# A two-layer graph network on one core: the table of k laid out by type, and key codes loaded for two blocks at once

## The chip, the cores and the metric

The kernel runs on one core of a Trainium2 chip. The core has five engines with an instruction queue each: TensorE (PE, matrix products, with its weight loads shown as PEld), VectorE (DVE), ScalarE (ACT), GpSimd (POOL) and SyncE (SP), which here only issues transfers. Sixteen DMA engines carry all transfers. A transfer is issued from the queue of SP or ACT (in the profile the hardware queues q1 and q10) or, where the addresses come from a list of row numbers, by POOL (an indirect transfer, queue q0). The metric is the time of one execution on the device in microseconds, lower is better.

## The reference

There are N = 30,000 nodes with 128 numbers each, and E = 960,000 edges (src, dst) sorted by destination. Layer 0 is a pair of relational convolutions, layer 1 a gated convolution with four edge types:

```python
# layer 0: 32 edge types, weights combined from 8 bases
W   = einsum('rb,bdf->rdf', coeff, basis)
msg = einsum('nd,rdf->nrf', h, W)[src, etype] * norm
agg = segment_sum(msg, dst)            # twice, relu between; x = x + result
# layer 1: T = 4 edge types
for t in range(T):
    k, q, v = x @ Wk[t] + bk[t], x @ Wq[t] + bq[t], x @ Wv[t] + bv[t]
    msg = sigmoid(k[dst] + q[src]) * v[src]
    msg = where(edge_type == t, msg, 0)
    outs.append(segment_sum(msg, dst) + x @ Ws[t] + b[t])
return x_in + mean(outs)               # x here is relu(layernorm(x_in))
```

## The kernel before

The kernel checks first that the destinations are sorted closely enough; then `sorted_path` runs (the other branch, `any_path`, is in the program but is not executed with these inputs). It passes over all edges three times: c1 and c2 for the two convolutions of layer 0, g for the gate of layer 1. A pass works on groups of 384 edges (three tiles of 128), 2500 of them. Five groups are a block (S = 5), five blocks a stage, twenty stages an iteration of 500 groups, and a hardware loop does five iterations. Because edges are sorted, the destinations of one group lie in a window of W = 32 consecutive nodes; `first` holds where each window starts. The sums stand in SBUF as `agg`, feature by node.

Between c2 and g the kernel does not stop: while c2 goes on, `after_second` takes finished nodes, 120 at a time, and writes for each node the four types' k (with the biases of k and q added) into the DRAM table `ktab`, and q and v into `qvtab` (stores at L817 from ACT, 480 rows of 512 bytes and 480 rows of 1024 bytes). In `ktab` the row of node n and type t is n * 4 + t, so a window of 32 nodes is 128 consecutive rows. During c1, `codes` writes two lists for the gate: `qidx` (src * 4 + type, the rows to gather from `qvtab`) and `kcode` (node within the window * 4 + type, bfloat16, one per edge; L890).

The gate pass (`gate_body`) does this for each group n:

- three indirect gathers by POOL, of 128 rows of 1 KB each, fetch q and v of the edges' sources into `qv` (L119, ten groups' buffers). A gather is issued when the buffer of ten groups before has been read;
- SP loads the window of k, 64 KB, into `kw` (L651, ten buffers), five groups ahead of the group that POOL is at; its start comes from a register that SP read from `first`;
- three products by PE of a one-hot matrix `oh` with `kw` give each edge its k, `pk` (`keys`, L668); they are issued one group ahead;
- DVE adds q (L709), ACT takes the sigmoid in place (L710), DVE multiplies by v two groups later into `msg` (L677), and three products by PE with the selection matrix `sel` sum the messages by window (L679);
- once per block, DVE makes the next block's `oh` (L655, 128 x 1920, from the key codes `kb`, comparing them with the partition's number) and `sel` (L661), and adds the last block's windows into `agg` (L470).

`kb` holds the key codes of one block, broadcast to all 128 partitions by a load of 480 KB (L644, 128 rows of 3840 bytes, two buffers). It is issued at the first group of block s for block s + 1 and takes the place of block s - 1's codes, last read by the `oh` that DVE makes at group 1 of block s - 2. At the first group of a stage, SP also loads `qi` (row numbers for POOL), `relc` and `firsts` for the next stage. Every ten groups a node step copies finished sums out (`after_third`: L846 on ACT, L850 on PE, L853 on ACT, store L856).

The order on each queue is written out by hand (`manual_schedule`); waits between engines are semaphores that the framework derives. The gathers use five semaphores in turn, and a gather waits for the one five before it. Within SP's queue, kw loads, kb loads and stage loads stand in program order, and SP runs ahead of the other engines as far as the buffers allow.

The first pass has a load of a similar shape: `er`, the types of a block's edges, is read with an outer dimension of four, a broadcast over 32 and 2 KB rows (L512, 256 KB).

Of the kernel before, what the change touches and what calls it, by code (L numbers as in the profile page):

```python
# [9 lines left out]
F32 = mybir.dt.float32  # L10
# [9 lines left out]
P = 128  # L20
# [53 lines left out]
def kernel(  # L74
# [33 lines left out]
    h1 = nc.dram_tensor("h1", (NX, D), F32, kind="Internal").ap()  # L108
    agg1 = nc.dram_tensor("agg1", (NA, D), F32, kind="Internal").ap()
    agg2 = nc.dram_tensor("agg2", (NA, D), F32, kind="Internal").ap()  # L110
    ktab = nc.dram_tensor("ktab", (NX * T, D), F32, kind="Internal").ap()
    qvtab = nc.dram_tensor("qvtab", (NX * T, 2 * D), F32, kind="Internal").ap()
    reld = nc.dram_tensor("reld", (TP, NT), F32, kind="Internal").ap()
    kcode = nc.dram_tensor("kcode", (E,), BF16, kind="Internal").ap()
# [205 lines left out]
    def node_tables(pool, ps, wall, ball, hn, krows, qvrows):  # L320

        pt = ps.tile([P, P], F32, name="pt")
        nc.tensor.transpose(pt, hn, ident)
        hT = pool.tile([P, P], F32, name="hT")
        nc.scalar.activation(hT, pt, AF.Relu)
        kt = pool.tile([P, T, D], F32, name="kt")
        qvt = pool.tile([P, T, 2, D], F32, name="qvt")
        to = (kt, qvt[:, :, 0, :], qvt[:, :, 1, :])
        for a in range(3):
            pw = ps.tile([P, T, D], F32, name="pw", bufs=4)  # L330
            nc.tensor.matmul(pw.rearrange("p t f -> p (t f)"), lhsT=hT,
                             rhs=wall[:, a].rearrange("p t f -> p (t f)"), start=True, stop=True)
# [4 lines left out]
        nc.scalar.dma_start(krows, kt.rearrange("p t f -> p (t f)"))  # L337
        nc.sync.dma_start(qvrows, qvt.rearrange("p t a f -> p (t a f)"))
        return hT

    knode = ktab.rearrange("(n t) f -> n (t f)", t=T)
    qvnode = qvtab.rearrange("(n t) f -> n (t f)", t=T)


    def sorted_path():
# [7 lines left out]
        with ExitStack() as all_:  # L353
# [105 lines left out]
                    min_val=0, max_val=N - 1, skip_runtime_bounds_check_because=IN_RANGE)  # L459
                return vals  # L460

            def edge_row(row, i, s, n):

                return bass.AP(tensor=row.tensor, offset=(i * NG + s * S) * GE,
                               ap=[[0, n], [GE, S], [1, GE]])

            def add_windows(po, base, s, at=0):
                for g in range(S):
# [164 lines left out]
            def gate_body(i, io, pool, ps, cp, iw, ic, beside):  # L633
                stage = {}
                kb, oh, kw, sel, pk, qv, po, base, kbase = {}, {}, {}, {}, {}, {}, {}, {}, {}

                def loads(k):
                    got = [stage_tile(io, "qi", qidx, I32, i, k), firsts(io, i, k),
                           stage_tile(io, "relc", reld, F32, i, k)]
                    stage[k] = [got[1], got[0], got[2]]  # L640

                def types(s):
                    kb[s] = pool.tile([P, S, GE], BF16, name="kb")
                    nc.sync.dma_start(kb[s], edge_row(kcode, i, s, P))  # L644

                def window(n):
                    k = n // NGS
                    if n % NGS == 0:
                        kbase[k] = bases(stage[k][0], SP)
                    kw[n] = pool.tile([P, D], F32, name="kw", bufs=10)  # L650
                    nc.sync.dma_start(kw[n], ktab[ds(kbase[k][n % NGS] * T, P), :])  # L651

                def onehot(s):
                    oh[s] = pool.tile([P, S, GE], F32, name="oh")
                    nc.vector.tensor_tensor(oh[s], kb[s],  # L655
                                            ic.unsqueeze(2).to_broadcast([P, S, GE]),
                                            ALU.is_equal)
                    sel[s] = pool.tile([TP, S * G, W], F32, name="sel", bufs=3)
                    t0 = s % SB * S * G
                    relc = stage[s // SB][2][:, t0:t0 + S * G]  # L660
                    nc.vector.tensor_tensor(  # L661
                        sel[s], iw[:TP].unsqueeze(1).to_broadcast([TP, S * G, W]),
                        relc.unsqueeze(2).to_broadcast([TP, S * G, W]), ALU.is_equal)

                def keys(n):
                    pk[n] = ps.tile([TP, G, D], F32, name="pk", bufs=4)
                    for j in range(G):
                        nc.tensor.matmul(pk[n][:, j, :],  # L668
                                         lhsT=oh[n // S][:, n % S, j * TP:(j + 1) * TP],
                                         rhs=kw[n], start=True, stop=True)  # L670

                def sums(n):
                    s, g = n // S, n % S
                    if g == 0:
                        po[s] = ps.tile([P, S, W], F32, name="po")
                    msg = pool.tile([TP, G, D], F32, name="msg", bufs=3)
                    nc.vector.tensor_mul(msg, pk[n], qv[n][:, :, 1, :])  # L677
                    for j in range(G):
                        nc.tensor.matmul(po[s][:, g, :], lhsT=msg[:, j, :],  # L679
                                         rhs=sel[s][:, g * G + j, :],  # L680
                                         start=(j == 0), stop=(j == G - 1))

                loads(0)
                types(0)
                for n in range(S):
                    window(n)
                onehot(0)
                keys(0)
                for n in range(NG):
                    s, g, k = n // S, n % S, n // NGS  # L690
                    if n % NGS == 0:
                        if k in BEGINS:
                            tc.stage_boundary()
# [13 lines left out]
                    if n + 1 < NG:  # L707
                        keys(n + 1)
                    nc.vector.tensor_add(pk[n], pk[n], qv[n][:, :, 0, :])  # L709
# [12 lines left out]
                add_windows(po[NS - 1], base[NQ - 1], NS - 1)  # L722
# [36 lines left out]
            def after_second(weights):  # L759

                def steps(at, pool, ps, deep):
# [63 lines left out]
                    def own():  # L825
# [6 lines left out]
                            (7, biased(1, qvt[:, :, :D])), (7, weight(2)), (7, part),  # L832
                            (8, biased(2, qvt[:, :, D:])), (8, own),
                            (9, store(nc.sync if isinstance(at, int) else nc.scalar,
                                      qvnode, qvt)))
                return steps

            def after_third(weights):
# [22 lines left out]
            def codes(i, pool):  # L861
# [8 lines left out]
                def part(h):  # L870
# [38 lines left out]
    def any_path():  # L909
        with ExitStack() as all_:  # L910
# [112 lines left out]
            with tc.tile_pool(name="snodew", bufs=1) as nodew, \  # L1023
# [8 lines left out]
                with tc.For_i(0, NB, 1) as i:  # L1032
                    xt = node.tile([P, 1, D], F32, name="xt")
                    nc.sync.dma_start(xt[:, 0, :], agg2[ds(i * P, P), :])
                    hn = normalised(node, xt, 1, "snode")
                    hT = node_tables(node, nps, wall, ball, hn[:, 0, :], knode[ds(i * P, P), :],
                                     qvnode[ds(i * P, P), :])
                    po = nps.tile([P, D], F32, name="po")
                    nc.tensor.matmul(po, lhsT=hT, rhs=wsm, start=True, stop=True)
# [5 lines left out]
            with tc.tile_pool(name="gslow", bufs=2) as pool, \  # L1045
# [7 lines left out]
                nc.vector.scalar_tensor_tensor(ki, di, float(T), e4, op0=ALU.mult, op1=ALU.add)  # L1053
                k = pool.tile([TP, G, D], F32, name="k")
                qv = pool.tile([TP, G, 2 * D], F32, name="qv")
                for j in range(G):
                    gather(qv[:, j, :], qvtab[:NP * T, :], qi[:, j:j + 1])
                    gather(k[:, j, :], ktab[:NP * T, :], ki[:, j:j + 1])
# [80 lines left out]
```

## Time and profile before

Ten runs: median 33253.57 us (33241.48 to 33262.07). The profiled execution took 33250.78 us.

| What | us |
|---|---|
| profiled execution, its own time | 33250.78 |
| its span, first to last instruction | 33248.9 |
| first pass, first to last gather | 159 to 11029 |
| second pass | 11055 to 21847 |
| gate pass | 21886 to 33225 |
| POOL busy, whole span | 21332.0 (64%) |
| PE busy | 19752.3 (59%) |
| PE weight loads | 16299.6 (49%) |
| DVE busy | 11504.8 (35%) |
| ACT busy | 3590.1 (11%) |

In the profile's lines, `out<-in` names the tiles of the program, `x` a number of instructions, and after `<-` stands what ended an engine's wait. "issue" means that the profile shows nothing that was waited for, "remote" that the release came from a semaphore event with no instruction's end near it. SPq and ACTq are the queues that issue transfers. The times of PE's matmuls are modelled, so PE's real completions are read from what waits for them.

### The profile page before, as it was taken

The page shows a single profiled execution, that of the slowest core. Times are in us where ns is not written, and L with a number is a line of the kernel's source. Part 1 is how long each engine was busy: PE and PEld are TensorE (multiplying, and loading weights), DVE is VectorE, ACT ScalarE, POOL GpSimd, SP SyncE. Part 2 cuts the span into 40 slices and gives each one's busy share as a digit, 9 for nine tenths or more (in the row PEclk, how much of TensorE's full clock was granted, in tenths as well). Part 3 has the DMA queues.
Part 4 walks back from the last instruction along what each step waited for, and adds up shares of the span by engine and source line. Part 5 has one row for each costly group of instructions (what it writes and reads, how often), then busy time and mean ns, then how long its engine had stood idle before and what let it go on. Part 6 is the DMA issues. An engine that isn't in the chain of part 4 may idle for free. (4 is left out here: it accounts for less than half of the span.)

```text
span 33248.9 us, 278474 instructions
## 1 busy us (share of the span) xinstructions
PE 19752.3 (59%) x79371; PEld 16299.6 (49%) x79371; DVE 11504.8 (35%) x23672; ACT 3590.1 (11%) x9806; POOL 21332.0 (64%) x22514
## 2 busy tenths in 40 slices
PE   4555555555555566666666666655555555555565
PEld 3444444444444444444444444445555555555555
DVE  4333333333333333333333333333333333333333
ACT  2000000000000111111111111111111111111111
POOL 5666666666666666666666666666666666666666
PEclk8777777777777787887888888865555555555555
DMA  3222222222222222222222222234444444444444
GB/s 110 65 65 71 65 70 66 65 72 65 68 68 65 64 67 66 67 68 66 66 67 67 67 66 67 67 107 126 125 125 126 125 126 126 124 126 126 125 126 121
DMA packets 1982877, 2920.57 MB, mean 88 GB/s; under 512 B 680564, under 2 KB 1364077, under 8 KB 1981277
## 3 DMA queue, kind: packets, MB, share of 16 engines
q0 software_dynamic: 840000, 1967.52, 22.0%
q1 hardware_dynamic: 740695, 661.98, 6.8%
q10 hardware_dynamic: 400582, 272.46, 2.8%
q8 instruction: 672, 11.01, 0.1%
q14 instruction: 928, 7.60, 0.1%
HBM read 2626.82 MB, written 273.30 MB: 87 GB/s over the span
## 5 line engine op out<-in xcount | busy, mean ns | idle before, releaser
L119 POOL DMA_INDIRECT hg<-h,idx x15000 | 14194.7, 946 | 7624.1 <-issue 4203.4
L605 PE MATMUL pa<-sb,hg 128*128 128x256 f32 x30000 | 9110.0, 460 | 6472.0 <-issue 5223.7
L605 PEld LDWEIGHTS pa<-sb,hg 128*128 128x128 f32 x30000 | 6737.2, 234 | 8568.0 <-issue 5906.3
L119 POOL DMA_INDIRECT qv<-qvtab,qi x7500 | 7110.1, 948 | 4268.0 <-issue 2054.9
L679 PE MATMUL po<-sel,msg 128*128 128x32 f32 x15000 | 3455.8, 386 | 4568.6 <-DVE msg L677 4174.0
L679 PEld LDWEIGHTS po<-sel,msg 128*128 128x128 f32 x15000 | 3429.1, 328 | 4854.3 <-DVE msg L677 4330.8
L668 PE MATMUL pk<-kw,oh 128*128 128x128 f32 x15000 | 3998.4, 439 | 57.1 <-DVE oh L655 46.8
L609 ACT COPY ab<-pa 128x256 f32<-128x256 f32 x5000 | 1802.2, 373 | 19528.6 <-remote 9954.2
L709 DVE TENSOR_TENSOR pk<-pk,qv 128x384 f32<-128x384 f32 x2500 | 1406.5, 563 | 7026.4 <-remote 4728.8
L668 PEld LDWEIGHTS pk<-kw,oh 128*128 128x128 f32 x15000 | 3478.8, 331 | 57.7 <-issue 57.7
L470 DVE TENSOR_TENSOR agg<-agg,pb 128x32 f32 x5000 | 937.8, 188 | 6491.9 <-remote 5369.3
L555 PE MATMUL pb<-ab,bas 128*128 128x160 f32 (+1 forms) x12080 | 2571.9, 369 | 554.9 <-ACT ab L609 358.6
L555 PEld LDWEIGHTS pb<-ab,bas 128*128 128x128 f32 x12080 | 2071.3, 205 | 1046.6 <-issue 406.1
L601 DVE TENSOR_TENSOR sb<-cp,ce 128x768 f32<-128x768 f32 x2500 | 2320.8, 949 | 693.8 <-remote 496.5
L601 DVE TENSOR_TENSOR sb<-hits,ce 128x768 f32<-128x768 f32 x2500 | 2294.9, 951 | 255.0 <-issue 164.9
L710 ACT ACTIVATE pk<-pk 128x384 f32<-128x384 f32 x2500 | 1187.3, 475 | 7700.6 <-DVE pk L709 4720.2
L801 PE MATMUL bank<-wall,hT 128*120 128x512 f32 x1518 | 975.5, 762 | 893.9 <-ACT hT L797 376.7
L677 DVE TENSOR_TENSOR msg<-pk,qv 128x384 f32<-128x384 f32 x2500 | 1369.7, 548 | 11.7 <-remote 10.2
L784 DVE BATCH_NORM_STATS2 st<-bank 120x6 f32<-120x128 f32 x253 | 75.6, 299 | 3321.6 <-remote 1489.1
L655 DVE TENSOR_TENSOR oh<-kb,cp 128x1920 f32<-128x1920 bf16 x500 | 1072.5, 2145 | 21.8 <-DMA kb<-kcode 15.8
L801 PEld LDWEIGHTS bank<-wall,hT 128*120 128x120 f32 x1518 | 324.9, 227 | 1190.9 <-issue 502.1
L812 DVE TENSOR_TENSOR kt<-bank,ball 120x512 f32<-120x512 f32 x253 | 175.0, 692 | 1775.1 <-PE bank L801 776.6
(83 smaller groups left out, 5486.2 us busy)
## 6 DMA issues: line engine op xcount, KB each, us to landing
hg<-h,idx POOLq DMA_INDIRECT x15000
kb<-kcode SPq DMA_DIRECT2D x500, 480.0 KB
kw<-ktab SPq DMA_DIRECT2D x2500, 64.0 KB
er<-in_et_row SPq DMA_DIRECT2D x500, 256.0 KB
qvtab<-qvt ACTq DMA_DIRECT2D x250, 480.0 KB
qv<-qvtab,qi POOLq DMA_INDIRECT x7500
ktab<-kt ACTq DMA_DIRECT2D x253, 240.0 KB
ce<-ce ACTq DMA_DIRECT2D x500, 60.0 KB
```

The costliest lines, as they stand in the source:

```text
L119: nc.gpsimd.indirect_dma_start(out=to, out_offset=None, in_=table, in_offset=bass.IndirectOffsetOnAxis(ap=idx, axis=0))
L555: nc.tensor.matmul(po[z][:, of].rearrange("p s w -> p (s w)"), lhsT=bas[:, b, :], rhs=ab[z][:, b, of].rearrange("p s w -> p (s w)"), start ...
L601: nc.vector.tensor_mul(sb, hits[:, of, :].unsqueeze(2).to_broadcast([TP, G, B, W]), ce[s][:, of, :].unsqueeze(3).to_broadcast([TP, G, B, W]))
L605: nc.tensor.matmul(pa.rearrange("p b w -> p (b w)"), lhsT=hg[:, j, :], rhs=sb[:, j].rearrange("p b w -> p (b w)"), start=(j == 0), stop=(j ...
L609: nc.scalar.copy(ab[z][:, :, s % A * S + g, :], pa)
L655: nc.vector.tensor_tensor(oh[s], kb[s], ic.unsqueeze(2).to_broadcast([P, S, GE]), ALU.is_equal)
L668: nc.tensor.matmul(pk[n][:, j, :], lhsT=oh[n // S][:, n % S, j * TP:(j + 1) * TP], rhs=kw[n], start=True, stop=True)
L677: nc.vector.tensor_mul(msg, pk[n], qv[n][:, :, 1, :])
L679: nc.tensor.matmul(po[s][:, g, :], lhsT=msg[:, j, :], rhs=sel[s][:, g * G + j, :], start=(j == 0), stop=(j == G - 1))
L709: nc.vector.tensor_add(pk[n], pk[n], qv[n][:, :, 0, :])
L710: nc.scalar.activation(pk[n], pk[n], AF.Sigmoid)
L801: nc.tensor.matmul(bank(a, VB, T * D), lhsT=hT, rhs=wall[:, a].rearrange("p t f -> p (t f)"), start=True, stop=True)
```

## The change

Two things change in the gate pass, and the tables it reads change with them.

- `ktab` becomes a table of four planes, type then node: (T, NX, D) instead of (NX * T, D). A window load reads, for each of the four types, 32 consecutive nodes, so the source of `kw` has three dimensions, 4 x 32 x 128, and partition t * 32 + w of `kw` holds type t of window node w. The store of k writes each node's four rows into four planes. The key code becomes type * 32 + node within the window, which is made by the same DVE operation with its two operands exchanged.
- `kb` holds the codes of two blocks. It is loaded at the first group of every even block, for the pair of blocks after, as 128 rows of 7680 bytes (960 KB), and each block's one-hot reads its half.

```diff
-    ktab = nc.dram_tensor("ktab", (NX * T, D), F32, kind="Internal").ap()
+    ktab = nc.dram_tensor("ktab", (T, NX, D), F32, kind="Internal").ap()
...
-    knode = ktab.rearrange("(n t) f -> n (t f)", t=T)
+    knode = ktab.rearrange("t n f -> n t f")
...
-            def edge_row(row, i, s, n):
+            def edge_row(row, i, s, n, groups):
                 return bass.AP(tensor=row.tensor, offset=(i * NG + s * S) * GE,
-                               ap=[[0, n], [GE, S], [1, GE]])
+                               ap=[[0, n], [GE, groups], [1, GE]])
...
-                def types(s):
-                    kb[s] = pool.tile([P, S, GE], BF16, name="kb")
-                    nc.sync.dma_start(kb[s], edge_row(kcode, i, s, P))
+                def types(z):
+                    kb[z] = pool.tile([P, 2 * S, GE], BF16, name="kb")
+                    nc.sync.dma_start(kb[z], edge_row(kcode, i, 2 * z, P, 2 * S))
...
-                    nc.sync.dma_start(kw[n], ktab[ds(kbase[k][n % NGS] * T, P), :])
+                    nc.sync.dma_start(kw[n], ktab[:, ds(kbase[k][n % NGS], W), :])
...
-                    nc.vector.tensor_tensor(oh[s], kb[s],
+                    nc.vector.tensor_tensor(oh[s], kb[s // 2][:, s % 2 * S:s % 2 * S + S],
                                             ic.unsqueeze(2).to_broadcast([P, S, GE]),
                                             ALU.is_equal)
...
-                    if g == 0 and s + 1 < NS:
-                        types(s + 1)
+                    if g == 0 and s % 2 == 0 and s + 2 < NS:
+                        types(s // 2 + 1)
...
-                            queue.dma_start(
-                                table[rows, :].rearrange("p (t f) -> p t f", t=T), t)
+                            queue.dma_start(table[rows], t)
...
-                        nc.vector.scalar_tensor_tensor(kc, kr, float(T), er, op0=ALU.mult,
+                        nc.vector.scalar_tensor_tensor(kc, er, float(W), kr, op0=ALU.mult,
                                                        op1=ALU.add)
```

The rest of the diff is the same layout in `any_path`, which is not executed.

More of the change, by code (lines that the diff above doesn't have):

```diff
@@ L336, in node_tables @@
                 nc.vector.tensor_add(to[a], pw, ball[:, a])
-        nc.scalar.dma_start(krows, kt.rearrange("p t f -> p (t f)"))
+        nc.scalar.dma_start(krows, kt)
         nc.sync.dma_start(qvrows, qvt.rearrange("p t a f -> p (t a f)"))
         return hT
-    knode = ktab.rearrange("(n t) f -> n (t f)", t=T)
+    knode = ktab.rearrange("t n f -> n t f")
     qvnode = qvtab.rearrange("(n t) f -> n (t f)", t=T)
@@ L834, in steps @@
                             (9, store(nc.sync if isinstance(at, int) else nc.scalar,
-                                      qvnode, qvt)))
+                                      qvnode.rearrange("n (t f) -> n t f", t=T), qvt)))
                 return steps
@@ L1035, in any_path @@
                     hn = normalised(node, xt, 1, "snode")
-                    hT = node_tables(node, nps, wall, ball, hn[:, 0, :], knode[ds(i * P, P), :],
+                    hT = node_tables(node, nps, wall, ball, hn[:, 0, :], knode[ds(i * P, P)],
                                      qvnode[ds(i * P, P), :])
@@ L1052, in any_path @@
                 ki = pool.tile([TP, G], I32, name="ki")
-                nc.vector.scalar_tensor_tensor(ki, di, float(T), e4, op0=ALU.mult, op1=ALU.add)
+                nc.vector.scalar_tensor_tensor(ki, e4, float(NX), di, op0=ALU.mult, op1=ALU.add)
                 k = pool.tile([TP, G, D], F32, name="k")
@@ L1057, in any_path @@
                     gather(qv[:, j, :], qvtab[:NP * T, :], qi[:, j:j + 1])
-                    gather(k[:, j, :], ktab[:NP * T, :], ki[:, j:j + 1])
+                    gather(k[:, j, :], ktab.rearrange("t n f -> (t n) f"), ki[:, j:j + 1])
                 s = pool.tile([TP, G, D], F32, name="s")
```

## The prediction

> **What bounds the kernel now.** I read the page first, then the three passes over the edges as three stretches, then the gate pass alone: the order of its instructions around one block, and what the queue of SP waits for.
>
> The costliest groups of the page; after the bar come busy time, mean of one, and the idle time ahead of it:
>
> ```profile
> L119 POOL DMA_INDIRECT hg<-h,idx x15000 | 14194.7, 946 | 7624.1 <-issue 4203.4
> L119 POOL DMA_INDIRECT qv<-qvtab,qi x7500 | 7110.1, 948 | 4268.0 <-issue 2054.9
> ```
>
> The three passes (stretch, its length, then busy time of PE, weight load, DVE, ACT, POOL; granted clock; DMA share; GB/s):
>
> ```profile
> 159.00:11029.00 10870.00, 6193.28 (x27475) 5269.69 (x27476) 3498.28 (x7294) 999.61 (x2997) 7100.59 (x7500) 0.74 0.26 67
> 11055.00:21847.00 10792.00, 6794.04 (x21541) 4561.87 (x21542) 3656.90 (x7230) 1163.94 (x3495) 7093.45 (x7500) 0.80 0.26 67
> 21886.00:33225.00 11339.00, 6725.95 (x30164) 6440.31 (x30165) 4195.56 (x8471) 1305.46 (x2998) 7110.06 (x7500) 0.51 0.43 126
> ```
>
> Each pass issues 7500 gathers and lasts 1.45, 1.44 and 1.51 us per gather. A gather cannot follow the last sooner than 0.948 + 0.305 = 1.253 us (the timeline's even steps), so POOL without stalls would need 9.40 ms a pass. The gate pass, which the change is about, is 1.94 ms above that. Its timeline shows where one block (5 groups, 15 gathers) loses them:
>
> ```profile
> 30007.13 0.69 SPq L644 DMA_DIRECT2D kb<-kcode  x1
> 30007.36 1.40 PEld L668 LDWEIGHTS pk<-kw,oh 128*128 128x128 f32 x6
> 30007.43 1.63 PE L668 MATMUL pk<-kw,oh 128*128 128x128 f32 x6
> ...
> 30012.68 0.95 POOL L119 DMA_INDIRECT qv<-qvtab,qi  x1 [0.30 <-issue]
> 30015.61 0.27 ACT L853 COPY o<-pr 120x128 f32<-120x128 f32 x1 [9.48 <-remote]
> 30016.40 11.57 SPq L651 DMA_DIRECT2D kw<-ktab  x5
> 30016.41 0.57 DVE L709 TENSOR_TENSOR pk<-pk,qv 128x384 f32<-128x384 f32 x1 [9.34 <-remote]
> 30016.88 0.55 DVE L677 TENSOR_TENSOR msg<-pk,qv 128x384 f32<-128x384 f32 x1
> ...
> 30017.70 0.95 POOL L119 DMA_INDIRECT qv<-qvtab,qi  x1 [4.07 <-DVE msg L677]
> ```
>
> POOL runs 15 gathers, fills its ten qv buffers, stops at 30013.63 and goes on at 30017.70. The transposition pr that ACT waits for had run on PE at 30004; keys for the DVE's add had run by 30006. Their completions reach ACT, SP and DVE only at 30015.6 to 30016.4, after POOL has stopped and its transfers have ended (DMA share 0.01 from 30014.9 to 30016.4). So while gathers flow, PE's completions are seen ever later, in steps of about 0.7 us (14.89, 15.58, 16.30 in the trace's semaphore records); when the gathers stop they come in a burst. The stall: 1.26 of drain, 1.52 of completions, 1.29 for the add, the product and POOL's restart: 4.07. The block: 15 x 1.253 + 4.07 - 0.30 = 22.56 us. Of the pass's 502 stalls over 2 us, 478 follow the last by exactly 15 gathers. The first two passes, without kb and kw, do the same: stalls of 3.0 to 3.5 us, mostly 15 gathers apart in the first, 9 to 24 in the second.
>
> SP's queue in the gate pass, from 23000 to 32900:
>
> ```profile
> SPq L651 <- remote: 2085.0, 386, 10.9
> SPq L651 <- PE pk L668: 1641.9, 491, 5.0
> SPq L651 <- PE po L679: 1278.0, 440, 5.7
> SPq L644 <- DVE oh L655: 45.2, 2, 23.9
> ```
>
> SP waits 5.0 of 9.9 ms for kw buffers: it is a whole ring of ten windows ahead. The last kw is issued near 33205, its keys run near 33233.
>
> **The change, part by part.** The profiled execution took 33250.78 us: passes 33001, the rest 250. The ten runs' median is 33253.57, 2.8 above.
>
> *Key codes, 500 loads of 480 KB to 250 of 960 KB.* Removed from SP: 250 x (0.696 issue + 0.712 MOVE + 0.08 registers and wait) = 372 us. The bytes stay. A load of 480 KB takes DMA share 0.84 for 2.30 us (282 GB/s, from 30007.0); the double takes about 4.6. It is issued one block in two and may start under the old condition: its buffer's last reader is the one-hot of block s-1, which DVE does in block s-2. That wait exists now: 45 us, twice. Behind it on SP stand the kw loads and the stage's qi, relc and firsts; POOL waits for qi and PE for kw, qi loaded a stage of five blocks ahead and kw some 28 us. On the path: 0, covered by SP's lead. Without that lead a late load would hold the one-hot, at up to 4.6 us x 250 = 1.15 ms. A gain is bounded by the stalls of the 250 blocks that lose their load: 250 x 3.77 = 943 us. I take 0, because the second pass has no such load and stalls all the same.
>
> *kw with an outer dimension of four, 2500 loads.* No row is a load of 128 rows of 512 B in four parts. The nearest is er of the first pass: 128 rows, four outer, 0.565 us on SP against kw's 0.333, and four completion writes in the packet records where kw posts sixteen. So +0.232 x 2500 = 580 us on SP; with the 372 saved, SP gains 208 us of work against 5 ms of waiting: 0 on the path. er's packets run 3.4 us after the first; kw's now about 0.6 to 1.1. By 512-byte packets (27.6 ns each) a ring that had 8 rows, 0.22 us, now has 32, 0.88. Landing comes later by 0.7 (bounds 0 and er's 3.4 - 0.6 = 2.8), covered by a lead of some 28 us. Per block those four rings carry gathers 30 x 0.219 = 6.6, kw 5 x 0.88 = 4.4, kb 8 x 0.195 = 1.6: 12.6 of 22.6 us, not full. Completion writes per block go from 240 + 80 + 16 = 336 to 240 + 20 + 8 = 268. If they were what delays PE's completions, this would gain; the bounds are 0 and one step of 0.7 us a block, 350 us. I take 0: blocks that carry the stage's loads (33 writes more, every fifth) last 22.6 us like the others (medians 22.56 to 22.63 over ten kinds of block).
>
> The Trainium skill ("DMA: Bandwidth & Descriptors", on why a DMA increments its semaphore by 16, and its rules for kernel authors) says that the engines used are the largest number up to 16 that divides both outer sizes, and warns that an outer dimension under 16 confines the transfer. The er packets agree with the first part. The rule speaks against this edit: by the page's ~27 GiB/s per engine an estimate is 0.14 us on sixteen and 0.57 on four, and 2500 x 0.43 = 1.07 ms, 34.3 ms in all, if every load were waited for. The rows say that none is.
>
> *Stores of ktab* (second pass, 253): 480 rows of 512 B before and after, since the tile's rows are padded; 0.906 us each on ACT. Bound 0 to 253 x 0.16 (the row's maximum of 1.07) = 41 us on an engine busy 11%: 0. *Key code arithmetic*: the same 20 DVE operations of 548 ns with two operands exchanged: 0; bound their whole 11 us. *The one-hot* reads half a tile, 1920 elements a row as before: 0.
>
> Sum: 33250.8 + 0.
>
> **Rivals.** A change of 0.2% (66 us, 0.13 us a block) is about what this kernel's measurement tells from none.
>
> A, no change: the stall is set by gathers alone. That kw still used sixteen rings would end here too. 33,250.
>
> B, faster: the blocks without kb leave the fixed step. For it: after a kb load PE's completions come most slowly (in one recorded block 9.9, 14.1, 19.8 us after the restart). Against: the second pass. Price: that pass's 1.439 us per gather instead of 1.512, in half the gate's gathers, 3750 x 0.073 = 274: 32,980; at most 943.
>
> C, faster: fewer completion writes save a step of 0.7 us in each block, 350: 32,900. Against: the stage blocks.
>
> D, slower: the double burst. A gather waits for the one five before it (five semaphores in turn), so it may land 6.26 us after its issue; it takes 2.5 now, margin 3.8. During 480 KB four gathers' completions already come as one train. If gathers get nothing for 4.6 us, POOL waits 0.8, and the backlog lengthens the drain by up to a gather's 1.25: 250 x 0.8 to 2.05, 200 to 510 us, middle 33,600. It decides from a lag of 3.8 us on. Against: the packets of both queues alternate.
>
> E, slower: gathers end late on the four rings; 0.88 us of kw ahead of the last gather of a block at most, and SP issues none while POOL stands. 500 x 0.3 (a third of it): 33,400.
>
> **How the numbers follow.** A 0.32, B 0.22, C 0.14, D 0.22, E 0.10: faster 0.36, same 0.32, slower 0.32. A's own range is 33,185 to 33,320. The range reaches from half of B's bound below (450 us) to the middle of D above: 32,800 to 33,600; outside lie the far ends of B and D, under 2 in 10.
>
> **What would show it.** A: kw posts 4 completion writes, its issue near 0.56 us; kb x250; the stall of POOL stays at 4.1 us every 15 gathers and the gate pass at 11.34 ms. B: blocks alternate, one near 22.6, one near 19 to 21. C: all blocks shorter by 0.7. D: POOL's wait for qv's DMA, 18.9 us now, grows to hundreds, in the blocks with kb. E: gathers land later in every block. The step most likely wrong is that kb and kw are idle riders of a stall that gathers alone make.

## The result and the profile after

The changed kernel takes 33485.73 us (median of 8 runs) against 33252.74 us for the kernel before beside it: a ratio of 1.0070, 95% interval 1.0061 to 1.0079. It is slower by 233 us. The forecast was 33,250 with a range of 32,800 to 33,600: the time lies in the range, the likeliest case (no change) was wrong. The profiled execution took 33482.37 us, its span is 33480.6.

The three passes, in the same stretches as before (stretch, its length, busy time of PE, weight load, DVE, ACT, POOL; granted clock; DMA share; GB/s):

```profile
159.00:11029.00 10870.00, 6177.68 (x27478) 5295.87 (x27478) 3492.91 (x7294) 1000.41 (x2997) 7081.69 (x7500) 0.74 0.26 67
11055.00:21847.00 10792.00, 6799.47 (x21589) 4561.60 (x21590) 3663.20 (x7262) 1172.51 (x3509) 7074.96 (x7500) 0.80 0.26 67
21886.00:33225.00 11339.00, 6620.32 (x29530) 6329.40 (x29531) 4110.61 (x8293) 1274.08 (x2933) 6934.26 (x7338) 0.51 0.41 123
```

In the first two stretches POOL issues its 7500 gathers as before. In the third it reaches 7338: 162 are left when the old pass would have ended. From its first gather to the end of its last the gate pass went from 11338.5 to 11586.8 us, which is 1.512 to 1.545 us per gather: +248. It begins 20 us earlier, because the second pass took 20 us less (10771.7 us from its first gather to the end of its last, 10791.3 before). That pass holds the store of `ktab`, whose issue on ACT fell from 0.906 to 0.353 us; on the two chips of the later runs that show the stalls described below and ran both stores (e1 to e4, e5 to e12) it is 2 to 29 us shorter with the new one, one trace a run, so a small gain there is likely and not shown.

POOL's rows add up to the 248: its stalls over 2 us went from 2069 to 2267 us (+198), its pauses of 0.6 to 2 us from 31 to 149 (+118), and gathers and short pauses took 67 less. What POOL waits for in the gate pass (in all, times, longest), first the kernel before, then the changed one:

```profile
POOL qv L119 <- DVE msg L677: 1736.5, 443, 15.7
POOL qv L119 <- DVE agg L470: 31.2, 77, 4.7
POOL qv L119 <- DMA qv<-qvtab,qi: 18.9, 57, 0.8
```

```profile
POOL qv L119 <- DVE msg L677: 1625.0, 426, 15.3
POOL qv L119 <- DVE agg L470: 212.1, 78, 5.1
POOL qv L119 <- DMA qv<-qvtab,qi: 63.9, 122, 2.6
```

The wait is still the one for DVE's product, and behind a product that is late, DVE's additions to agg. The wait for a gather's own landing rose by 45 us, a small part. DVE's wait for keys is where it starts: the group L709 waited 4151.7 us for "remote" between 23000 and 32900 before, and 4903.7 after.

The stalls themselves changed in two ways. Before, 478 of 502 came 15 gathers after the last. Now 316 of 564 do, and 188 come after 12, 38 after 3. And those after 15 are longer: median 4.57 us instead of 4.10. The trace's records split such a stall: gathers still end 1.49 us after POOL stops (1.48 before), but PE's completions, which come in one burst, start 3.10 us after it instead of 2.68. A stall after 12 is shorter (3.55 us on the mean) but dearer per gather: 3.55 / 12 = 0.30 us against 4.08 / 15 = 0.27 before.

The loads of kw, instruction by instruction (count, then shortest / median / longest in ns), before and after:

```profile
L651 SPq FUSED_REGOPS  x2500: 2/46/1408, 21888.2 to 33200.8; - x193
L651 SPq DMA_DIRECT2D kw<-ktab x2500: 3/333/712, 21888.5 to 33205.0; - x193
```

```profile
L651 SPq FUSED_REGOPS  x2500: 2/37/1394, 21868.1 to 33428.7; - x193
L651 SPq DMA_DIRECT2D kw<-ktab x2500: 2/532/994, 21868.4 to 33435.9; - x193
```

One issue takes 532 ns instead of 333. The hardware queue of SP carries 674695 packets instead of 740695; of the 66000 fewer, 30000 are completion writes of kw (2500 x 12), four a load instead of sixteen, and 36000 belong to the 250 loads of kb that are gone (128 packets and 16 writes each). So the change does what it says, and what follows is about why that costs 0.7%.

### The profile page after: what moved, and what is told of

The parts are those of the page before. It is cut to its first block, busy times and chain, and to the rows that moved or that the text cites. A ratio compares the mean times of both kernels' runs of the same rounds, so it can differ in the third digit from the quotient of the medians.

```text
span 33480.6 us, 277532 instructions
## 1 busy us (share of the span) xinstructions
PE 19769.0 (59%) x79371; PEld 16345.1 (49%) x79371; DVE 11504.4 (34%) x23672; ACT 3592.9 (11%) x9806; POOL 21272.9 (64%) x22514
## 3 DMA queue, kind: packets, MB, share of 16 engines
q1 hardware_dynamic: 674695, 661.84, 6.4%
## 5 line engine op out<-in xcount | busy, mean ns | idle before, releaser
L709 DVE TENSOR_TENSOR pk<-pk,qv 128x384 f32<-128x384 f32 x2500 | 1407.1, 563 | 7280.8 <-remote 5753.2
```

## The experiments

Each ratio is against the kernel before on the same chip, since chips differ: it took 33548.54 us beside e1 to e4, 33509.50 beside e5, e9, e11 and e12, 33224.81 beside f5, 33532.50 beside f6. Beside the others it took about 28,440, of which more below.

In what follows a ring is one DMA engine's share of a queue, counted by the completion writes of a load: four or sixteen. The letters of the theories are those of the experiments, and where a rival of the prediction is meant, the text says so. The first theories were K, four rings instead of sixteen; C, the double burst of key codes; L, the layout, whose source in three dimensions takes SP longer to issue. L was then split into S, SP's time, and F, the form of the transfer itself; Q is S with a mechanism, by way of the 0.70 us steps. Last, F was split into G, a source in pieces, and A, rows in four planes. "In pieces" means here that the rows do not follow each other at one even distance, so that the source keeps its third dimension.

### Which part costs

e1 merges the key codes and leaves the table alone.

```diff
-                    kb[s] = pool.tile([P, S, GE], BF16, name="kb")
-                    nc.sync.dma_start(kb[s], edge_row(kcode, i, s, P))
+                    kb[z] = pool.tile([P, 2 * S, GE], BF16, name="kb")
+                    nc.sync.dma_start(kb[z], edge_row(kcode, i, 2 * z, P, 2 * S))
```

> Only the key codes are changed: 250 loads of 960 KB, the table of k and its loads as before. Theory K (the loads of k with four outer rows cause the loss, because they run on four rings): 33,250, within 30 us of before. Theory C (the double burst of the codes causes it): about 33,485, +0.7%. Theory L (the source with three dimensions and SP's longer issue cause it): 33,250.

Measured: 33544.99 us, ratio 0.9999 (0.9989 to 1.0008). The merged codes cost nothing and gain nothing, so theory C falls.

e2 has the table by type and the loads with an outer dimension of four, with the old key code loads.

```diff
-                    nc.sync.dma_start(kw[n], ktab[ds(kbase[k][n % NGS] * T, P), :])
+                    nc.sync.dma_start(kw[n], ktab[:, ds(kbase[k][n % NGS], W), :])
```

> Only the table of k is changed: planes by type, loads of k with an outer dimension of four; codes loaded block by block as before. Theory K: about 33,485, with a stall of POOL above 4.1 us and 4 completion writes for each load of k. Theory C: 33,250. Theory L: about 33,485.

Measured: 33817.08 us, ratio 1.0079 (1.0062 to 1.0096). This half carries the whole loss, 269 us.

e3 keeps the table by type, but reads it node by node, 32 x 4 x 128, so that sixteen rings take part; the key code stays what it was.

```diff
-                    nc.sync.dma_start(kw[n], ktab[ds(kbase[k][n % NGS] * T, P), :])
+                    nc.sync.dma_start(kw[n], ktab[:, ds(kbase[k][n % NGS], W), :].rearrange("t w f -> w t f"))
```

> The table of k in planes by type, but each load takes the window's node as the outer dimension (32 x 4 x 128), so partition and key code are node * 4 + type as before, and the source still has three dimensions; codes block by block. It tells the rings from the layout. Theory K: 16 completion writes for each load and 33,250, within 30 us. Theory C: 33,250. Theory L: SP's issue stays near 0.53 us, and about 33,485.

Measured: 33707.84 us, ratio 1.0047 (1.0030 to 1.0064); sixteen completion writes a load, and still 538 ns of issue. So sixteen rings save 109 us against e2 and the larger part of the loss stays: K can explain the smaller part at most.

e4 is e3 with the merged key codes.

> As the run before it, and codes for two blocks at once: the whole change except the four rings. Theory K: 33,250 within 30 us. Theory C: about 33,485. Theory L: about 33,485. If the halved number of code loads is worth something once the rings are sixteen, some us under 33,250.

Measured: 33685.21 us, ratio 1.0040 (1.0025 to 1.0054), like e3. In three pairs (before and e1, e2 and the changed kernel, e3 and e4) merging the codes moves nothing that can be told.

### Rings, SP's time, or the form of the load

e5 was to have four rings in the old layout.

```diff
-                    nc.sync.dma_start(kw[n], ktab[ds(kbase[k][n % NGS] * T, P), :])
+                    nc.sync.dma_start(kw[n], ktab[ds(kbase[k][n % NGS] * T, P), :].rearrange("(a b) f -> a b f", a=4))
```

> Everything as before, but the source of each load of kw is written as 4 x 32 x 128 over the same 128 contiguous rows. K (four rings): four completion writes a load, SP's issue still 0.333 us, and the difference between e2 and e3 alone, ratio about 1.003. S (the time that SP spends on a load) and F (a source in separate pieces): 1.000. If the loads still post sixteen writes, the source was taken as one piece, and the run says nothing on K.

Measured: 33501.49 us, ratio 0.9998 (0.9989 to 1.0008), issue 333 ns. Its SP queue posts 44454 four-byte writes between 23000 and 32900 for 2168 loads of kw and the other loads of that time; before, 44744 for 2180. So a load still posts sixteen: the adjoining rows were taken as one piece, and the run says nothing on four rings.

e9 moves the changed kernel's kw loads to ACT's queue.

```diff
-                        kbase[k] = bases(stage[k][0], SP)
+                        kbase[k] = bases(stage[k][0], mybir.EngineType.Activation)
...
-                    nc.sync.dma_start(kw[n], ktab[:, ds(kbase[k][n % NGS], W), :])
+                    nc.scalar.dma_start(kw[n], ktab[:, ds(kbase[k][n % NGS], W), :])
```

> The changed kernel, with its kw loads and their base registers on ACT's queue instead of SP's (ACT is 89% idle). S: SP issues no kw any more, so the part of the loss that e3 shows (0.47%) goes and K's 0.3% stays: ratio about 1.003; ACT's sigmoid may come later by an issue of 0.53 us, which would add up to 500 x 0.5 = 250 us. F: the loads are what they were, ratio 1.007 as for the changed kernel.

Measured: 33682.84 us, ratio 1.0050 (1.0033 to 1.0067), between the two expectations. It needed its partner, f5 below.

e11 loads each window of the new table by four loads of 32 adjoining rows.

```diff
-                    nc.sync.dma_start(kw[n], ktab[:, ds(kbase[k][n % NGS], W), :])
+                    for t in range(T):
+                        nc.sync.dma_start(kw[n][t * W:(t + 1) * W, :],
+                                          ktab[t, ds(kbase[k][n % NGS], W), :])
```

> The changed kernel, with each window loaded by four loads of 32 contiguous rows instead of one load with an outer dimension of four. S: four issues of about 0.33 us, 1.33 us a step instead of 0.53; at e3's rate (0.47% for 0.21 us more) the 1.0 us more than before gives 2.2%, ratio about 1.02. F: each load is in one piece, ratio about 1.000; K: sixteen rings, 1.000. More completion writes (64 a window instead of 16) would count with S.

Measured: 33931.20 us, ratio 1.0127 (1.0110 to 1.0144); 10000 issues of 315 ns. F's 1.000 fails: loads in one piece cost too when there are four times as many. S's 1.02 fails in size: 0.93 us more of issue for a group cost 1.27%, where e3's 0.205 us cost 0.47%.

e12 was to add SP time without a transfer.

```diff
+                    nc.values_load_multi_w_load_instructions(
+                        stage[k][0][:, :4], engines=[SP], min_val=0, max_val=N - 1,
+                        skip_runtime_bounds_check_because=IN_RANGE)
```

> The kernel before, with four more register loads on SP ahead of each load of kw, whose values are not used: no transfer is added. S: some 0.2 to 0.3 us more of SP a step gives what e3 gives, ratio 1.004 to 1.007. F and K: 1.000.

Measured: 33542.86 us, ratio 1.0010 (1.0001 to 1.0020). The register loads, whose values are not used, are not in the trace; all that was added is one semaphore instruction a group, 17 ns at the median. So it is no test of 0.2 us of SP. It shows that the pattern is easily tipped: 248 stalls came after 12 gathers, against 47 in e5 on the same chip.

### Two chips without stalls

The next eight runs met two chips on which the kernel before takes 28456.60 and 28418.59 us, and on which POOL's pauses over 2 us all but vanish: none to six in a gate pass. What the edits are:

e10 (and f2, f5): the kernel before with its kw loads and base registers on ACT's queue, as e9 has them. e13: fourteen qv buffers instead of ten. e14 (and f3): one kw tile for a block's five windows.

```diff
-                    kw[n] = pool.tile([P, D], F32, name="kw", bufs=10)
-                    nc.sync.dma_start(kw[n], ktab[ds(kbase[k][n % NGS] * T, P), :])
+                    if n % S == 0:
+                        kw[n // S] = pool.tile([P, S, D], F32, name="kw", bufs=3)
+                    nc.sync.dma_start(kw[n // S][:, n % S, :], ktab[ds(kbase[k][n % NGS] * T, P), :])
```

e15 (and f4): the changed kernel with that kw tile. f1: the changed kernel as it is.

> The kernel before, with its kw loads and their base registers on ACT's queue: the partner of e9. Q (the loss is made on SP: once gathers have run for some 11 us, SP's instructions and PE's completions come one at a time, 0.70 us apart, so whatever SP does then delays the DVE's add): with SP rid of kw, the layout matters no more, and this run comes out like e9, ratio 1.004 to 1.006, both paying for ACT's issues ahead of the sigmoid. F (the transfer's own form, three-dimensional and on four rings): this run is faster than e9 by the loss of the change, 0.7%, ratio about 0.998.

> The kernel before, with fourteen qv buffers instead of ten. POOL could run up to 12 gathers more before it stops for a buffer. If the drain of the gathers is what lets PE's completions through, a stall of about 4.1 us comes every 27 gathers instead of every 15: 7500 x (4.1/15 - 4.1/27) = 910 us less, ratio 0.973. If completions come late in proportion to how long the gathers have run, the stall grows with the run and nothing is gained: ratio 1.000. F says nothing of it.

> The kernel before, with one kw tile of five windows per block (three of them) instead of ten tiles of one window: the same 2500 loads, but SP waits for PE once per block instead of once per load. Q: SP has four instructions fewer per block and issues the five loads together, so fewer fall among PE's completions: from e12 (five instructions more per block, 0.1% slower) a gain of 0.1% if only their number counts, ratio 0.999, more (0.99) if SP then issues in the time in which POOL stands. F: 1.000.

> The changed kernel with the same edit as e14. Q: what the change costs shrinks with the instructions of SP that fall among PE's completions: within 0.3% of e14. F: the loads are the same as in the changed kernel, so this is 0.7% above e14.

> The changed kernel as it is, so that it stands beside the others on one chip. On a chip whose gate pass stalls as in the profile before (some 500 stalls over 2 us): ratio 1.007, as first measured. On a chip without these stalls (as in the runs of e10, e13, e14 and e15, where the kernel before took 28457 us): Q has no steps in which SP and PE could meet, and expects 1.000 to 1.001; F expects the transfers to cost the same there, but hidden behind POOL: 1.000 to 1.002.

> As e10, where stalls occur. Q: like e9, ratio 1.004 to 1.006, because what then costs is ACT's issues and no longer the layout. F: 0.998, that is 0.7% below e9.

> As e14, where stalls occur. Q: 0.999 if only the number of SP's instructions counts, 0.99 if SP then issues while POOL stands. F: 1.000.

> As e15, where stalls occur. Q: within 0.3% of f3. F: 0.7% above f3, like the changed kernel above the kernel before.

| run | us | ratio | 95% |
|---|---|---|---|
| e10, kw on ACT | 28467.05 | 1.0004 | 0.9994 to 1.0013 |
| e13, fourteen qv | 28460.26 | 1.0001 | 0.9992 to 1.0011 |
| e14, kw by block | 28469.02 | 1.0004 | 0.9995 to 1.0014 |
| e15, changed, kw by block | 28496.00 | 1.0013 | 1.0003 to 1.0022 |
| f1, changed | 28466.74 | 1.0017 | 1.0008 to 1.0027 |
| f2, kw on ACT | 28431.40 | 1.0005 | 0.9995 to 1.0014 |
| f3, kw by block | 28426.05 | 1.0003 | 0.9993 to 1.0013 |
| f4, changed, kw by block | 28455.16 | 1.0014 | 1.0004 to 1.0023 |

The stretch of f3's gate pass, columns as above:

```profile
18995.00:28375.00 9380.00, 7250.79 (x30214) 6582.69 (x30214) 4280.27 (x8484) 1287.59 (x3003) 7086.57 (x7497) 0.50 0.52 152
```

Here the pass takes 1.251 us per gather, which is gather and pause and nothing else: no stall over 2 us. PE's keys reach DVE at once. f3's additions in the timeline (start, length; in brackets the idle time before and what ended it):

```profile
25003.26 0.57 DVE L710 TENSOR_TENSOR pk<-pk,qv 128x384 f32<-128x384 f32 x1 [2.69 <-PE pk L669]
25007.09 0.57 DVE L710 TENSOR_TENSOR pk<-pk,qv 128x384 f32<-128x384 f32 x1 [1.83 <-PE pk L669]
25010.40 0.57 DVE L710 TENSOR_TENSOR pk<-pk,qv 128x384 f32<-128x384 f32 x1 [2.28 <-DMA qv<-qvtab,qi]
```

The additions follow each other after 3.8 and 3.3 us, and none waits for "remote". SP's plain instructions tell the two kinds of chip apart. On f3's chip and f1's (shortest / median / longest ns):

```profile
L652 SPq FUSED_REGOPS  x2500: 46/46/51, 18996.9 to 28323.9; - x193
```

```profile
L651 SPq FUSED_REGOPS  x2500: 37/37/47, 18995.3 to 28381.3; - x193
L651 SPq DMA_DIRECT2D kw<-ktab x2500: 532/532/1985, 18995.7 to 28384.3; - x193
```

Where POOL stalls, the same register instruction takes up to 1408 ns (the line of before above): of SP's moves and register operations in the gate pass of the kernel before, 1303 of 6592 take over 0.6 us, most of them about 0.7 and most 10 to 18 us after POOL went on, in the time in which PE's completions are also late. On the chips without stalls none does.

The traces of the two kinds of chip differ in one more way. In every run a gather posts 16 completion writes (the four-byte packets of q0). On the chips without stalls the trace has a semaphore event for 15.9 to 16.0 of them, on the chips with stalls for 2.2 to 2.9, and there the engines' own events are fewer too: 11660 of PE's 15206 and 4642 of DVE's 8590 are in the gate pass of the kernel before, against 15218 of 15238 of PE's in f3. Whether these events come merged or are only lost to the record is not shown. Every execution timed here has a recorded span and clock, so whether the recording itself has a part in the stalls is open as well. The late completions do not rest on the semaphore events alone: DVE's late starts show them.

So eight runs told nothing on F or Q, and one thing of its own: with the stalls gone, the longer issue of kw, 532 ns here too, costs next to nothing. What f1 loses, 48 us, is another term: its pauses over 0.6 us are 70 with 72 us in all (12 with 13 us in f3), 57 of them end 6 to 10 us after an issue of kb (in f3, with single loads, all 12 do), and POOL waits there for its own gather:

```profile
POOL qv L119 <- DMA qv<-qvtab,qi: 135.9, 303, 2.1
```

This is the mechanism of the prediction's rival D in small: about 1 us, after a quarter of the 250 double loads. e15 (31 of 56 pauses so placed) and f4 (16 of 35) have it less clearly, and no run on these chips had the double codes alone, so that the codes rather than kw make it is likely and not shown.

### SP, or the load itself

> The kernel before with kw on ACT's queue once more, for a chip on which the gate pass stalls. Q: like e9, ratio 1.004 to 1.006. F: about 0.998, 0.7% below e9. On a chip without stalls it tells nothing new (1.0004 and 1.0005 there).

Measured on a chip with stalls: 33218.94 us, ratio 0.9999 (0.9990 to 1.0008). With kw on ACT, the old layout costs nothing and the new one costs 0.50% (e9, on another chip and with the double codes, which cost nothing in e1). F's 0.998 fails in size, since moving the loads gained nothing. ACT's rows of the two, e9 first:

```profile
L651 ACTq DMA_DIRECT2D kw<-ktab x2500: 4/540/1155, 22062.5 to 33677.0; - x193
```

```profile
L651 ACTq DMA_DIRECT2D kw<-ktab x2500: 3/339/1673, 21867.3 to 33188.2; - x193
```

So Q falls: the loss does not need SP's queue. Nor do the stalls: in f5 SP has a quarter of its instructions left (1591 moves and register operations, 6592 before), and POOL's stalls over 2 us are 525 with 1978 us, against 502 with 2069.

f6 keeps the old table and only fetches a window's 128 adjoining rows in another order.

```diff
-                    nc.sync.dma_start(kw[n], ktab[ds(kbase[k][n % NGS] * T, P), :])
+                    nc.sync.dma_start(kw[n], ktab[ds(kbase[k][n % NGS] * T, P), :].rearrange("(a b) f -> b a f", a=8))
```

> The kernel before with its old table, one load per window of the same 128 adjoining rows, but fetched in the order 16 x 8 (row 16a + b to partition 8b + a), which is a source in pieces on sixteen rings. The key codes are not reordered to match, so the rows of k that are multiplied are the wrong ones: that part of the computation is left out, and every instruction and byte remains. G (the load costs because its source is in pieces): SP's issue 0.53 us and, where the gate pass stalls, a ratio near e3's 1.0047. A (it costs because its rows lie in four planes far apart in memory): 1.000. On a chip without stalls both expect 1.000 to 1.001, and only the issue time tells anything.

Measured: 33713.33 us, ratio 1.0053 (1.0039 to 1.0066). G holds and A falls: same bytes, same 64 KB, same sixteen rings, the same number of packets to the last one as in the kernel before (740695), and the loss of e3. The transfer itself is no slower: its 512-byte packets take 27.1 ns on the mean against 27.6, and those of a load that stands alone spread over 0.57 us against 0.55 (medians). What differs is the issue, and that the first packet starts 1.34 us after it began instead of 1.00. The issue and POOL's timeline:

```profile
L651 SPq DMA_DIRECT2D kw<-ktab x2500: 2/540/1547, 22075.5 to 33675.3; - x193
```

```profile
30010.66 0.94 POOL L119 DMA_INDIRECT qv<-qvtab,qi  x1 [2.83 <-DVE agg L470]
...
30024.40 0.95 POOL L119 DMA_INDIRECT qv<-qvtab,qi  x1 [0.30 <-issue]
30029.21 0.94 POOL L119 DMA_INDIRECT qv<-qvtab,qi  x1 [3.86 <-DVE msg L677]
...
30042.95 0.94 POOL L119 DMA_INDIRECT qv<-qvtab,qi  x1 [0.30 <-issue]
30047.97 0.94 POOL L119 DMA_INDIRECT qv<-qvtab,qi  x1 [4.07 <-DVE msg L677]
```

From 30010.66 to 30024.40 there are 12 gathers, then a stall, 12 more, a stall. In the kernel before 15 fit between two stalls, because DVE got through five groups; here it does four. DVE's additions in the kernel before, then in f6:

```profile
30016.41 0.57 DVE L709 TENSOR_TENSOR pk<-pk,qv 128x384 f32<-128x384 f32 x1 [9.34 <-remote]
30017.35 0.56 DVE L709 TENSOR_TENSOR pk<-pk,qv 128x384 f32<-128x384 f32 x1
30020.90 0.56 DVE L709 TENSOR_TENSOR pk<-pk,qv 128x384 f32<-128x384 f32 x1
30023.01 0.57 DVE L709 TENSOR_TENSOR pk<-pk,qv 128x384 f32<-128x384 f32 x1 [1.09 <-issue]
30027.64 0.57 DVE L709 TENSOR_TENSOR pk<-pk,qv 128x384 f32<-128x384 f32 x1 [3.61 <-PE pk L668]
30038.96 0.57 DVE L709 TENSOR_TENSOR pk<-pk,qv 128x384 f32<-128x384 f32 x1 [9.31 <-remote]
```

```profile
30027.92 0.57 DVE L709 TENSOR_TENSOR pk<-pk,qv 128x384 f32<-128x384 f32 x1 [9.92 <-remote]
30028.85 0.55 DVE L709 TENSOR_TENSOR pk<-pk,qv 128x384 f32<-128x384 f32 x1
30032.78 0.57 DVE L709 TENSOR_TENSOR pk<-pk,qv 128x384 f32<-128x384 f32 x1 [1.93 <-PE po L679]
30037.96 0.57 DVE L709 TENSOR_TENSOR pk<-pk,qv 128x384 f32<-128x384 f32 x1 [4.16 <-PE pk L668]
30046.68 0.57 DVE L709 TENSOR_TENSOR pk<-pk,qv 128x384 f32<-128x384 f32 x1 [5.07 <-remote]
```

In f6 the third and fourth additions after the burst have waited 1.93 and 4.16 us for PE, and the fifth is caught by the next stall. Over all stalls of a run, the fourth addition starts 5.31 to 5.33 us after POOL goes on where kw is in one piece (before, e1, e5, f5; medians) and 6.30 to 6.31 where it is in pieces (f6, e3, e4, e2, e9); the changed kernel and e12, with stalls of both kinds in number, lie between (5.41 and 5.74).

The counts, from the traces of the runs on chips with stalls. Burst is the time from POOL's stop to the first two of PE's completions that follow each other within 0.1 us, a median, for the stalls after 15 gathers and for those after 12. It rests on the semaphore events, but DVE's first addition, which does not, comes 1.29 us before POOL goes on in the median of the runs compared here, so the stall's length tells the same.

| run | kw | issue, us | after 15 / after 12 gathers | burst, us, after 15 / 12 | us per gather |
|---|---|---|---|---|---|
| before | one piece, SP | 0.333 | 478 / 17 | 2.68 / 2.21 | 1.512 |
| e5 | one piece, SP | 0.333 | 452 / 47 | 2.79 / 2.32 | 1.521 |
| e1 | one piece, SP, double codes | 0.333 | 455 / 35 | 2.84 / 2.30 | 1.525 |
| e12 | one piece, SP, one more semaphore instruction | 0.333 | 266 / 248 | 2.78 / 2.35 | 1.527 |
| f5 | one piece, ACT | 0.339 | 396 / 83 | 2.66 / 2.23 | 1.510 |
| f6 | pieces, 16 rings, SP | 0.540 | 118 / 426 | 3.05 / 2.54 | 1.549 |
| e3 | pieces, 16 rings, SP | 0.538 | 104 / 434 | 3.05 / 2.56 | 1.549 |
| e4 | pieces, 16 rings, SP, double codes | 0.538 | 137 / 391 | 3.01 / 2.56 | 1.544 |
| e2 | pieces, 4 rings, SP | 0.532 | 126 / 421 | 3.05 / 2.67 | 1.562 |
| after | pieces, 4 rings, SP, double codes | 0.532 | 316 / 188 | 3.10 / 2.59 | 1.545 |
| e9 | pieces, 4 rings, ACT, double codes | 0.540 | 174 / 344 | 2.65 / 2.58 | 1.549 |
| e11 | four loads of one piece, SP | 4 x 0.315 | 6 / 367, and 299 after 9 | 1.88 / 2.33 | 1.580 |

With kw in one load of one piece the chips differ by up to 0.015 us per gather, so the rows are to be read for their pattern. In all of them the gathers end 1.46 to 1.49 us after POOL stops, so the drain plays no part. Loads in pieces move stalls from 15 to 12 gathers on either queue, though e12 shows that other things do so too, and then at a price of 0.1%. On SP they also delay the burst by 0.2 to 0.4 us in both kinds of stall; on ACT the stalls after 15 show no delay (2.65 against 2.66), but those after 12, which are most of e9's, show the same 0.35 us (2.58 against 2.23).

## Why the prediction was wrong

The step that failed is "*kw with an outer dimension of four, 2500 loads*", and in it "with the 372 saved, SP gains 208 us of work against 5 ms of waiting: 0 on the path". The term put at 0 measured 269 us where it stood alone (e2), and 233 us with the rest of the change. Most of its pieces were right one by one. Issue: 0.565 taken from er, 0.532 measured. Completion writes: four. Landing: forecast 0.7 us later, measured some 1.1 (first packet 1.40 us after the issue began instead of 1.00, the packets spread over 1.27 us instead of 0.55), and covered: PE's wait list in the gate pass has no wait for kw, before or after. The 372 us were too many: kb's issue of 0.696 us and its MOVE of 0.712 are those of late instructions on a chip with stalls; in f3 the same two take 0.333 and 0.029. What was wrong is that the sum held only ways through SP's time and kw's landing. A load in pieces acts on the stall itself, and neither lead covers that: f6 has a cost of 0.53% with the same rows, bytes and number of rings.

The range of 32,800 to 33,600 holds the time, but it reached so far up for rival D, whose mechanism did not make the loss (e1). That is luck.

The argument that closed the question was "blocks that carry the stage's loads ... last 22.6 us like the others". Those loads are issued like the old kw (qi and relc at 0.333 and 0.350 us in f3, their rows at one even distance), and so was every row I had of SP's traffic in the gate pass. er is in pieces, and I used its duration as a price of SP's time, which had slack, and not as a mark that it is another kind of transfer.

The stall mechanism was right for the chip it was read on, and it is what the loss came through: the added 198 us stand in stalls, by PE's late completions and not by the drain. That gathers alone make the stall was right as far as SP goes (f5: kw gone from SP, and as many stalls), but it is not a property of the program: on two chips the same gathers run without any. The floor of 1.253 us per gather was right: they run at 1.251.

The rivals of the prediction. A fell by the 0.7%. B: even blocks, which hold the kb load, and odd blocks take 23.3 and 23.1 us after, on the mean; neither comes near the 19 to 21 forecast, and e1 gains nothing. C: 30,000 completion writes fewer, no gain. D: e1 is 0.9999 where POOL stalls; POOL's wait for qv's DMA rose to 63.9 us, not to hundreds. It appears in small only where there are no stalls (f1). E had the side and a size of 150 us against the 233 measured, by the wrong way: it lengthened the drain, which stayed. What four rings do is in e2 against e3: gathers early in a run land 2.6 to 3.1 us after issue instead of 2.4 to 2.7, and the time grows by 109 us, with intervals that just overlap.

The rule of the Trainium skill that I weighed ("DMA: Bandwidth & Descriptors", the rules for kernel authors) spoke against the edit. The estimate of 1.07 ms that I worked out from the page, if every load were waited for, is not what happened; e2 and e3 put the price of the rings nearer 0.1 ms. The four completion writes of the changed kernel's kw agree with the page's part on how many engines a transfer uses.

What stays open is by what path such a load delays PE's completions. SP's plain instructions and PE's completions both move in steps of about 0.7 us while gathers run, which suggests that something is shared, and a load in pieces or four loads instead of one (e11) seems to take more of it. Nor is it shown whether the form costs by its longer issue or in another way: f6 changes both together, e11 speaks for the time or the number of issues, and e12, which was to add time alone, added next to none. No run took that apart. Nor was any edit found that beats the kernel before: e13 and e14 were aimed at the stalls and met no chip that has them.

## What to carry to other kernels

Price a transfer by its form and not only by bytes, rings and queue time: where an issue's median went from 0.33 to 0.53 us here, the load was of another kind, and it cost although nobody waited for it. A covered step is covered only against the waits in the list; when the path hangs on late completions ("remote"), a load that joins that traffic may be on the path (kw in pieces was, the double codes were not), and the nearest row should be one of the same form. Look at the longest as well as the median of a plain instruction (46/46/51 against 2/46/1408): here it told whether a chip had the effect at all.

## What the hardware did that was not expected

- The same kernel takes 28.42 and 28.46 ms on two chips and 33.22 to 33.55 ms on the others, at nearly the same time per gather (0.945 to 0.948 us). The difference is POOL's stalls: none over 2 us in the gate pass of f3, 502 in the profile before. The effect of one and the same change is 1.0017 there and 1.0070 here.
- A load of 128 rows of 512 B from adjoining rows takes 0.333 us to issue on SP and 0.339 on ACT (medians); with its rows in pieces, over four planes or only in another order, 0.532 to 0.540 on either. Rows apart but at one even distance (qi, relc) issue like adjoining ones.
- On the chips with stalls the traces hold a semaphore event for 2.2 to 2.9 of the 16 completion writes of a gather, on the two others for nearly all.
- A source written as 4 x 32 over adjoining rows is still one piece (e5), with the issue and completion writes of the kernel before.
- The store of ktab takes 0.353 us to issue on ACT in the new layout, 0.906 in the old.
